# Attention with a mixture of experts on one core: the routed inner layer computed transposed, and the experts' pieces spread one or more to a round

## The chip, the cores and the metric

The kernel runs on one core of a Trainium2 chip. The time is device microseconds of one execution. A core has five instruction streams: PE (TensorE: it multiplies a moving operand by weights that a separate load, PEld, puts into the array), DVE (VectorE), ACT (ScalarE), POOL (GpSimd) and SP (it only issues transfers here). Each runs its own instructions in the order in which the program lists them and waits on the others through semaphores.

## The reference

One layer on 2048 tokens of width 512. `x` is normalised and goes two ways, and both results are added to `x`.

```python
# attention: 16 heads, each with two score maps, causal softmax
attn1, attn2 = softmax(mask(q1 @ k1.T * scale)) @ v, softmax(mask(q2 @ k2.T * scale)) @ v
f = (rfft(attn1, axis=time) - lambda_full * rfft(attn2, axis=time)) * gaussian_filter
attn = rms_norm(irfft(f)) * rms_weight * (1 - LAMBDA_INIT) @ Wout
# feed-forward: 8 experts of inner width 352, each token takes 2, and a shared one of width 704
logits = x @ gate_w.T                       # softmax, top 2, weights renormalised
y_e = (silu(x @ w1[e]) * (x @ w3[e])) @ w2[e]
y = sum over the 2 chosen e of weight * y_e
shared = (silu(x @ sw1) * (x @ sw3)) @ sw2
```

All of it is fp32. One fp32 multiplication shows in the trace as two passes, each a weight load and a matmul; a transpose on PE shows as one.

## The kernel before

The program has three parts: a start (normalisation, gate, queries and keys, and the shared expert of the first four tiles of 128 tokens), `middle` (attention, the rest of the shared expert and the routed experts) and `ending` (the filter in time as products on PE, the projection, the sums). The change touches `middle` almost alone. There PE, DVE, ACT, POOL and SP keep the order in which the Python code emits instructions, so the order is written out by hand.

**Attention as a stream.** Two heads make a group `g` (8 of them), and each has four chunks of 512 queries, `qc` from 3 down to 0. A chunk is a list of units: scores of one head against one block of 128 keys, for both maps, in a PSUM buffer of two banks `ps_s` (there are two such buffers). `Chunk.scores` (L761) lets ACT take the exponential into `pt` (L774), and for blocks on the diagonal POOL clears the upper triangle (L779). `Chunk.values` (L801) multiplies by `v` into `ps_o`; `Chunk.added` (L818) has DVE add up `pt` over the keys. Of a finished chunk, `sums` reduces the added `pt` on PE (`ps_sum`, L827), ACT copies it, and `finish` turns the values and the sums on PE (`ps_ot` L839, `ps_st` L840) and has DVE take the reciprocal (L842) and scale (L847); `put` (POOL, L856) stores the difference of both maps in `vd`. When all four chunks of a group are stored, `folded` does a first butterfly of the filter on POOL in seven steps.

**Rounds.** The stream has 544 units; a round is four, so there are 136, 17 to a group (counted here from round 0). The loop at the end of `middle` does in each round: scores of two units (a first burst), the values of earlier units, `sums` of a chunk that closes, scores of two more units, the other values, `finish`, then pieces of the experts' work, DVE's sums, and steps of `folded`.

**Experts as pieces.** `experts()` is a generator; each `next` emits a piece and yields its estimated PE time, and the round loop takes pieces while `worked / work_all` is behind the round's share. A routed expert works on 128 gathered rows (`xrow`, an indirect transfer that POOL issues two experts ahead), 36 of them in order `j`, with two buffers of up weights (`wu`) and two of down weights (`wd`), which SP refills. It has three pieces: `up_first` (the `w1` half, `xh`, then tanh on ACT L175 and a product on DVE L176), `up_third` (the `w3` half, `xg`, and a product on DVE L182), and a third one that holds the down layer of the expert before (`xy`, L201), this one's inner layer turned back (`ps_u`, L191: three transposes, and two copies by DVE, L193 and L194) and the next one's rows turned (`ps_x`, L159, copied by ACT, L161).

In the up layer (L168) the turned rows `xT` are the weights in the array and 352 columns of `w1` or `w3` move past them, so the result has tokens on the partitions; the down layer needs the inner width there, which is why it is turned back. The shared expert (`hidden`, L231) has the other form already: 128 columns of its weights stay in the array and the tokens move.

`xh`, `xg`, `ps_u`, `ps_x`, `xy`, `ps_sum`, `ps_ot` and `ps_st` share three PSUM buffers (`f_ps`). A new tile takes the buffer that came free first in the program's order, and its first matmul waits until the last reader of that buffer is done.

Of the kernel before, what the change touches and what calls it, by code (L numbers as in the profile page):

```python
# [32 lines left out]
FCH = ((0, 128), (128, 128), (256, 96))  # L33
# [29 lines left out]
def block_kernel(  # L63
# [85 lines left out]
    def expert(mp, fps, yp=None, stores=2, by_scalar=False):  # L149
# [14 lines left out]
        def up_half(w, xT, i, name):  # L164
            dst = bank([P, FI], name)
            for c in range(NE):
                o = (2 * c + i) * FI
                nc.tensor.matmul(dst, xT[:, c, :], w[:, o : o + FI], start=(c == 0), stop=(c == NE - 1))  # L168
            return dst

        def up_first(w, xT):

            h = up_half(w, xT, 0, "xh")
            s = mp.tile([P, FI], F32, tag="s", name="xtanh")
# [13 lines left out]
        def turned_back(u):  # L188
            ps = bank([P, NF, P], "ps_u")
            for ic, (i0, m) in enumerate(FCH):  # L190
                nc.tensor.transpose(ps[:m, ic, :], u[:, i0 : i0 + m], ident)  # L191
            uT = mp.tile([P, NF, P], F32, tag="uT", name="uT")
            nc.vector.tensor_copy(uT[:, :2, :], ps[:, :2, :])  # L193
            nc.vector.tensor_copy(uT[:96, 2, :], ps[:96, 2, :])  # L194
            return uT

        def down_products(pairs):
            y = bank([P, E], "xy")
            for n, (w, uT) in enumerate(pairs):
                for ic, (_, m) in enumerate(FCH):  # L200
                    nc.tensor.matmul(  # L201
                        y, uT[:m, ic, :], w[:m, ic * E : (ic + 1) * E],
                        start=(n == 0 and ic == 0), stop=(n == len(pairs) - 1 and ic == NF - 1),
                    )
            return y
# [9 lines left out]
        def down(pairs, *to):  # L215
            stored(down_products(pairs), *to)

        return up_first, up_third, up, turned_back, (down, down_products, stored), transposed
# [59 lines left out]
    with ExitStack() as pools:  # L278
# [215 lines left out]
        _, _, _, _, (_, _, stored), _ = expert(ep, eps, stores=EARLY)  # L494
# [63 lines left out]
    def middle(general):  # L558


        with ExitStack() as pools:
# [29 lines left out]
            def experts():  # L591
# [5 lines left out]
                _, _, _, _, (_, _, stored), _ = expert(sp, fps, mp, by_scalar=True)  # L597
# [33 lines left out]
                up_first, up_third, _, turned_back, (down, _, _), transposed = expert(rp, fps, mp, by_scalar=True)  # L631
                for i in range(2):
                    fetch_down(es[i], i, nc.sync)
                xT = transposed(xr.pop(0))
                yield 0.5
                for j in range(NR):
                    half = up_first(w_sb[j % 2][0], xT)
                    yield 2.4
# [323 lines left out]
            for i in range(0, len(stream), 4):  # L962
# [7 lines left out]
                while todo:  # L970
                    ended += values()
# [403 lines left out]
```

## Time and profile before

| | us |
|---|---|
| median of 3 runs | 1381.73 (1381.63 to 1382.18) |
| the profiled execution, its own time | 1382.72 |
| its span, first to last instruction | 1380.8 |
| PE busy in it | 1331.9 |
| DVE, ACT, POOL busy | 1005.4, 692.7, 598.3 |
| start / `middle` / `ending`, by the trace | 0 to 253 / 253 to 1263 / 1263 to 1381 |

The routed experts run from about 600 to 1263 us, 18.4 us each. A row of a group gives line, engine, operation, out<-in, shapes and count, then busy time, mean duration of one, and idle time of the engine just before. Matmuls overlap: the mean duration of one is more than what it adds when many follow each other, and the chain (start, length, what) or the starts in the timeline tell what a series takes.

### The profile page before, as it was taken

How to read it: one execution, taken by the hardware profiler on the slowest of the kernel's cores; microseconds unless marked ns; L12 is line 12 of the kernel's file. 1: busy time of each engine (PE TensorE's matmuls, PEld its weight loads, DVE VectorE, ACT ScalarE, POOL GpSimd, SP SyncE). 2: the span in 40 equal slices, each digit the busy share in tenths (PEclk: the TensorE clock that was granted, in tenths of full speed). 3: DMA queues.
4: the chain of work that ended last, by engine and by line, in shares of the span. 5: the costliest groups of instructions: out<-in, count | busy, mean ns of one | idle time of the engine just before them, and what ended most of it. 6: DMA issues, size and time to landing. Idle time of an engine off the chain costs nothing.

```text
span 1380.8 us, 20566 instructions
## 1 busy us (share of the span) xinstructions
PE 1331.9 (96%) x7472; PEld 620.8 (45%) x7472; DVE 1005.4 (73%) x1337; ACT 692.7 (50%) x853; POOL 598.3 (43%) x673
## 2 busy tenths in 40 slices
PE   7999999899999999998899999999999999999998
PEld 3444444333443344444445444544454454445543
DVE  7059881368777776868677888867698779877785
ACT  2311110365656565665566566666667666662321
POOL 0002222012301232136975755757467537632874
PEclk9999999999999999999999999999999999999999
DMA  9406672200210121255455655656656565448996
GB/s 376 167 16 192 189 213 64 87 19 16 78 46 31 47 73 63 81 158 159 149 178 171 200 185 175 179 176 191 200 161 202 190 202 188 170 164 277 179 223 149
DMA packets 74689, 206.58 MB, mean 150 GB/s; under 512 B 12028, under 2 KB 12192, under 8 KB 69200
## 3 DMA queue, kind: packets, MB, share of 16 engines
q1 hardware_dynamic: 61840, 177.62, 39.4%
q0 software_dynamic: 11216, 23.31, 8.1%
q10 hardware_dynamic: 1520, 4.23, 0.9%
q8 instruction: 62, 1.02, 0.3%
q14 instruction: 51, 0.42, 0.1%
HBM read 161.26 MB, written 43.85 MB: 149 GB/s over the span
## 4 chain that ended last, share of the span: by engine, by line
PE 67%; DVE 5%; POOL 3%; DMA 3%; issue 2%; SPq 2%; ACT 2%; ACTq 0%; DVEq 0%; POOLq 0%
PE ps_o L801 17%; PE ps_s L761 12%; PE wh L231 8%; PE xy L201 6%; PE xh L168 6%; PE xg L168 6%; PE wy L269 4%; SPq L669 2%; PE ps_sum L827 2%; DVE sum L818 2%; ACT pt L774 1%; PE po L1196 1%; PE ps_ot L839 1%; PE ps_x L159 1%; DMA kS<-parts_k 1%
## 5 line engine op out<-in xcount | busy, mean ns | idle before, releaser
L818 DVE TENSOR_TENSOR sum<-sum,pt 128x1024 f32<-128x1024 f32 (+2 forms) x576 | 623.4, 1131 | 24.2 <-ACT pt L774 10.7
L774 ACT ACTIVATE pt<-ps_s 128x1024 f32<-128x1024 f32 x544 | 528.1, 1027 | 173.5 <-PE ps_s L761 128.1
L779 POOL TENSOR_SCALAR_AFFINE_SELECT pt<-pt 128x256 f32<-128x256 f32 x256 | 174.9, 708 | 340.5 <-ACT pt L774 277.5
L801 PE MATMUL ps_o<-pt,vd 128*32 128x512 f32 (+3 forms) x2560 | 270.7, 542 | 4.0 <-POOL pt L779 3.9
L761 PE MATMUL ps_s<-qS,kS 64*128 64x512 f32 (+3 forms) x1280 | 209.9, 411 | 14.7 <-ACT pt L774 12.9
L761 PEld LDWEIGHTS ps_s<-qS,kS 64*128 64x128 f32 x1280 | 97.8, 186 | 169.2 <-ACT pt L774 90.2
L231 PE MATMUL wh<-xnT,wu 128*128 128x512 f32 (+1 forms) x352 | 151.4, 578 | 0.0
L801 PEld LDWEIGHTS ps_o<-pt,vd 128*32 128x32 f32 x2560 | 67.2, 110 | 134.5 <-issue 115.5
L473 POOL DMA_INDIRECT who<-pairs,slot x32 | 34.3, 1073 | 202.0 <-DVE pairs L470 100.9
L520 PE MATMUL ps_x<-xnT,wqk_sb 128*128 128x512 f32 x256 | 110.5, 593 | 0.0
L201 PE MATMUL xy<-wd,uT 128*128 128x512 f32 (+1 forms) x216 | 103.5, 616 | 4.0 <-DVE rcp L842 4.0
L231 PEld LDWEIGHTS wh<-xnT,wu 128*128 128x128 f32 x352 | 64.9, 192 | 72.4 <-issue 57.3
L856 POOL TENSOR_TENSOR vd<-o_n 128x128 f32<-128x128 f32 x60 | 37.9, 653 | 137.2 <-DVE o_n L847 129.8
L168 PE MATMUL xh<-wu,xT 128*128 128x352 f32 x288 | 94.5, 471 | 0.7 <-ACT xT L161 0.7
L168 PE MATMUL xg<-wu,xT 128*128 128x352 f32 x288 | 93.2, 466 | 0.0
L520 PEld LDWEIGHTS ps_x<-xnT,wqk_sb 128*128 128x128 f32 x256 | 48.4, 190 | 60.6 <-issue 60.6
L269 PE MATMUL wy<-wd,ws 128*128 128x512 f32 x160 | 73.6, 601 | 0.0
L168 PEld LDWEIGHTS xh<-wu,xT 128*128 128x128 f32 x288 | 52.2, 191 | 33.6 <-issue 7.8
L168 PEld LDWEIGHTS xg<-wu,xT 128*128 128x128 f32 x288 | 52.6, 190 | 32.1 <-issue 4.3
L210 ACT ACTIVATE y_sb<-xy,wcol 128x512 f32<-128x512 f32 x36 | 24.8, 688 | 83.6 <-PE xy L201 83.6
L1052 POOL DMA_INDIRECT res<-ys,slot x32 | 56.6, 1769 | 21.0 <-DMA res<-ysh 10.4
L537 ACT CAST hi<-turned 128x1024 fp32r<-128x1024 f32 x16 | 16.7, 1045 | 93.8 <-DVE turned L535 83.1
(239 smaller groups left out, 1405.3 us busy)
## 6 DMA issues: line engine op xcount, KB each, us to landing
wu<-in_wex_dram SPq DMA_DIRECT2D x40, 1408.0 KB
wd<-in_wex_dram SPq DMA_DIRECT2D x39, 768.0 KB
kS<-parts_k SPq DMA_DIRECT2D x128, 128.0 KB
qS<-parts_q SPq DMA_DIRECT2D x256, 64.0 KB
ys<-y_sb SPq DMA_DIRECT2D x36, 256.0 KB
parts_q<-hi SPq DMA_DIRECT2D x32, 256.0 KB
parts_k<-hi SPq DMA_DIRECT2D x16, 256.0 KB
parts_k<-turned SPq DMA_DIRECT2D x16, 256.0 KB
```

The source lines that it names most:

```text
L168: nc.tensor.matmul(dst, xT[:, c, :], w[:, o : o + FI], start=(c == 0), stop=(c == NE - 1))
L201: nc.tensor.matmul(y, uT[:m, ic, :], w[:m, ic * E : (ic + 1) * E], start=(n == 0 and ic == 0), stop=(n == len(pairs) - 1 and ic == NF - 1),)
L231: nc.tensor.matmul(dst, w_sb[o // WUP][0][:, o % WUP : o % WUP + P], x[:, c, :], start=(c == 0), stop=(c == NE - 1))
L269: nc.tensor.matmul(y, us[i][:, t * P : (t + 1) * P], w_sb[i // NF][1][:, i % NF * E : (i % NF + 1) * E], start=(i == 0), stop=(i == SCH - 1),)
L520: nc.tensor.matmul(ps[:, i, :], wqk_sb[st, qk][:, i, c, :], xnT[:, c, cols], start=(c == 0), stop=(c == NE - 1),)
L761: nc.tensor.matmul(to, k, queries[2 * g + h, qc][r, off : off + w], start=True, stop=not general)
L774: nc.scalar.activation(pt[:, :, used], ps[:, :, used], AF.Exp, scale=SCALE)
L779: nc.gpsimd.affine_select(out=part, in_=part, pattern=[[0, 2], [1, P]], compare_op=ALU.is_ge, fill=0.0, base=0, channel_multiplier=-1,)
L801: nc.tensor.matmul(self.o[r : r + 32, off:], vd[:, kb, v0 : v0 + 32], pt[:, s, :], start=first, stop=self.ended, skip_group_check=True,)
L818: nc.vector.tensor_add(to, to, pt)
L856: eng.tensor_add(vd[:, self.qc * TQ : (self.qc + 1) * TQ, v0 : v0 + 32], self.o_n[:, :, h, 0, :], self.o_n[:, :, h, 1, :],)
L1052: nc.gpsimd.indirect_dma_start(out=came[k], out_offset=None, in_=ys, in_offset=bass.IndirectOffsetOnAxis(ap=slot[:, step - 2, order[k] : o ...
```

## The change

The inner layer of a routed expert is computed transposed. `up_half` keeps 128 columns of `w1` or `w3` in the array and moves the 128 columns of `xT`, for three overlapping column blocks (0, 128 and 224; the down weights of the 32 columns that come twice are zero the second time). Its result has the inner width on the partitions, [128, 3, 128] in place of [128, 352], and goes into the down layer as it is; `turned_back` and its two DVE copies are gone. The third piece turns the next expert's rows first and then does the down layer of the expert before. In the loop, every round takes at least one piece, a round whose first values were those of fewer than two blocks (and in which no chunk closes) takes one between its two bursts of scores, the estimates per piece differ, and a round ahead of one with diagonal blocks does one step of `folded`, not two. The layout of the down weights, prepared on the host, follows the blocks.

```diff
-FCH = ((0, 128), (128, 128), (256, 96))
+FCH = (0, 128, FI - 128)
...
         def up_half(w, xT, i, name):
-            dst = bank([P, FI], name)
-            for c in range(NE):
-                o = (2 * c + i) * FI
-                nc.tensor.matmul(dst, xT[:, c, :], w[:, o : o + FI], start=(c == 0), stop=(c == NE - 1))
+            dst = bank([P, NF, P], name)
+            for ic, i0 in enumerate(FCH):
+                for c in range(NE):
+                    o = (2 * c + i) * FI + i0
+                    nc.tensor.matmul(dst[:, ic, :], w[:, o : o + P], xT[:, c, :], start=(c == 0), stop=(c == NE - 1))
             return dst
...
-        def turned_back(u):
-            ps = bank([P, NF, P], "ps_u")
-            for ic, (i0, m) in enumerate(FCH):
-                nc.tensor.transpose(ps[:m, ic, :], u[:, i0 : i0 + m], ident)
-            uT = mp.tile([P, NF, P], F32, tag="uT", name="uT")
-            nc.vector.tensor_copy(uT[:, :2, :], ps[:, :2, :])
-            nc.vector.tensor_copy(uT[:96, 2, :], ps[:96, 2, :])
-            return uT
...
-        def down_products(pairs):
+        def down_products(w, u):
             y = bank([P, E], "xy")
...
+            for ic in range(NF):
+                nc.tensor.matmul(y, u[:, ic, :], w[:, ic * E : (ic + 1) * E], start=(ic == 0), stop=(ic == NF - 1))
             return y
...
                 for j in range(NR):
                     half = up_first(w_sb[j % 2][0], xT)
-                    yield 2.4
+                    yield 2.8
                     u = up_third(w_sb[j % 2][0], xT, half)
...
-                    yield 2.4
-                    if j > 0:
+                    yield 2.8
+                    if j + 1 < NR:
+                        xT = transposed(xr.pop(0))
+                    if late:
                         down(*late)
                         fetch_down(es[j + 1], (j + 1) % 2, nc.sync)
-                    uT = turned_back(u)
-                    late = [(w_sb[j % 2][1], uT)], ys[j * P : (j + 1) * P, :], wcol[:, j : j + 1]
-                    if j + 1 < NR:
-                        xT = transposed(xr.pop(0))
                     if j == 1:
                         shared.append(True)
-                    yield 3.7
+                    yield 3.2 if late else 0.6
+                    late = w_sb[j % 2][1], u, ys[j * P : (j + 1) * P, :], wcol[:, j : j + 1]
...
-            work_all = (NT - 1 - EARLY) * ((2 * SCH - 1) * 3.45 / TQ + 5.2) + NR * 8.5 - 7.0
+            work_all = (NT - 1 - EARLY) * ((2 * SCH - 1) * 3.45 / TQ + 5.2) + NR * 8.8
...
+            def work():
+                nonlocal worked
+                worked += next(ex, work_all)
...
                 found = burst(units[:2])
-                ended = values()
+                n, ended = values()
                 for c in closing:
                     c.sums()
                     summed += 1
+                if n < 2 and not closing:
+                    work()
                 found += burst(units[2:])
...
-                while worked / work_all < (i + 4) / len(stream):
-                    took = next(ex, None)
-                    if took is None:
-                        break
-                    worked += took
+                while True:
+                    work()
                     added(later[:1])
                     later = later[1:]
+                    if worked / work_all >= (i + 4) / len(stream):
+                        break
...
-                for _ in range(0 if any(map(masked, units)) or not shared else 1 if len(ready) < 2 else 2):
+                if any(map(masked, units)) or not shared:
+                    steps = 0
+                else:
+                    steps = 1 if len(ready) < 2 or any(map(masked, stream[i + 4 : i + 8])) else 2
+                for _ in range(steps):
```

## The prediction

> **What bounds the kernel now.** I read the page first, then stretches of time, then the chain, then the timeline around each PE gap. The page's first two parts say that PE is the bound:
>
> ```profile
> PE 1331.9 (96%) x7472; PEld 620.8 (45%) x7472; DVE 1005.4 (73%) x1337; ACT 692.7 (50%) x853; POOL 598.3 (43%) x673
> ...
> PE   7999999899999999998899999999999999999998
> ```
>
> So the change is worth two things in `middle`: PE work added or removed, and PE gaps filled or opened. The stretches (length, busy time by engine, granted clock, DMA) show how little is idle, and that a gap costs twice: the clock falls after it.
>
> ```profile
> 600.00:800.00 200.00, 187.32 (x1281) 90.99 (x1283) 154.25 (x182) 120.04 (x147) 144.24 (x166) 0.97 0.55 173
> ...
> 770.00:780.00 10.00, 6.93 (x35) 2.34 (x34) 9.86 (x11) 3.53 (x5) 9.29 (x9) 0.83 0.33 87
> 900.00:910.00 10.00, 8.65 (x46) 3.01 (x39) 7.51 (x7) 6.76 (x8) 9.46 (x10) 0.83 0.55 148
> ```
>
> A mean of 0.83 over 10 us is 1.7 us lost, on top of the gap. The chain (start, length, what, count) gives the price of the forms: half an up layer in the old form, the three transposes, and the new form, which the last tile of the shared expert has in `ending` (128 columns of weights in the array, 128 moving):
>
> ```profile
> 844.79 0.33 PE ps_u L191 x3
> ...
> 1233.19 2.37 PE xg L168 x8
> ...
> 1296.19 3.59 PE wh L231 x32
> ```
>
> **The change part by part.**
>
> *Up layer.* A half had 4 products, so 8 passes of 352 columns: 2.37/8 = 0.296 us each. It gets 3x4 products, 24 passes of 128 columns. The 32 passes of the last fence took 0.112 each, with a new weight load for every pass, so a half takes 2.69: +0.32, times 72 halves +23.0. Where scores follow, the old half took 2.56 instead of 2.37 (848.79 on the chain); turned rows followed by scores take 0.53 for four instead of 0.44, so the new form pays such an end too, and I count none.
>
> *Transposes.* 36 x 0.33 = -11.9. The two DVE copies (0.42 and 0.28 by their groups) go; the DVE and ACT operations grow from 352 to 384 columns (by the shared expert's 384 rows 0.557 and 0.492 against 0.52 and 0.465). DVE has 0.63 us less per expert, hidden under PE; if that cover is gone it is a gain.
>
> The Trainium skill, "TensorE: Matmul & The Clock Gate", section "Back-to-back issue gap", speaks against this part: in streams of load and matmul pairs it gives 81 ns per matmul of 128 columns where the isolated gap is 56. If the 25 ns came on top of each of the 1728 new passes, the sum would be some 43 us higher, an estimate from that page; the fence above already is such a stream.
>
> *Rounds without a piece.* I followed the loop by its yields for both kernels. Before, rounds 87, 92, 97 and 102 get none, and then the scores wait for ACT. The timeline of PE at round 87:
>
> ```profile
> 901.20 0.73 PE L761 MATMUL ps_s<-qS,kS 64*128 64x512 f32 x4
> 902.86 0.50 PE L761 MATMUL ps_s<-qS,kS 64*128 64x512 f32 x2 [0.93 <-ACT pt L774]
> 903.78 0.50 PE L761 MATMUL ps_s<-qS,kS 64*128 64x512 f32 x2 [0.41 <-ACT pt L774]
> 904.21 3.25 PE L801 MATMUL ps_o<-pt,vd 128*32 128x512 f32 x16
> ```
>
> Two bursts of 0.67 took from 901.20 to 904.21: 1.67 lost. In the same way 1.71 at 937.41, 1.70 at 975.31 and 1.08 at 1014.29: 6.2. Two were followed by a half-speed window (900 to 910 and 940 to 950, both 0.83): 3.4. After the change every round has a piece: -9.6.
>
> *The piece between bursts.* In round 8 of each group the first values are one block:
>
> ```profile
> 313.24 0.64 PE L801 MATMUL ps_o<-pt,vd 128*32 128x256 f32 x8
> 314.20 0.50 PE L761 MATMUL ps_s<-qS,kS 64*128 64x512 f32 x2 [0.32 <-ACT pt L774]
> 315.11 0.50 PE L761 MATMUL ps_s<-qS,kS 64*128 64x512 f32 x2 [0.42 <-ACT pt L774]
> 315.59 1.06 PE L801 MATMUL ps_o<-pt,vd 128*32 128x512 f32 x8
> ```
>
> Eight such passes take 0.56 (940.45 to 941.01), so 315.59 - 313.80 - 0.67 = 1.1 is lost, seven times, and 0.6 at 941: -8.4. A piece of 2.7 covers it. The same rule acts in round 0, where nothing covers the first exponentials:
>
> ```profile
> 257.87 1.71 PE L761 MATMUL ps_s<-qS,kS 64*128 64x512 f32 x4 [2.23 <-ACT pt L774]
> ```
>
> `wh` moves there: -2.2, and one of two half-speed windows around it (0.81 and 0.85 in 250 to 270), -1.7. Bounds -2 to -5.
>
> *The third piece, turned round.* In a closing round the next free PSUM buffer after `ps_sum`'s is `ps_st`'s, which DVE must have read. Before, in round 69, `xy` came first and covered part of DVE's lag:
>
> ```profile
> 768.02 0.27 PE L840 MATMUL ps_st<-cst,s_sb 128*128 128x128 f32 x1
> 768.13 2.74 PE L201 MATMUL xy<-wd,uT 128*128 128x512 f32 x6
> ...
> 773.13 0.25 DVE L842 RECIPROCAL rcp<-ps_st 128x16 f32<-128x16 f32 x1
> 773.43 0.55 PE L191 MATMUL ps_u<-cst,xtanh 128*128 128x128 f32 x3 [2.56 <-DVE rcp L842]
> ```
>
> Afterwards only the rows (0.44) stand before `xy`, which waits about 4.5 from 768.5; the round takes 7.8 from `ps_st`, not 7.1, and without the transposes should take 6.8: +1.0, and one more half-speed window +1.7. DVE's lighter work does not help, since it idled at 756.49 just before this backlog. Rounds 111 and 119 meet the same order with lags of 1.3 (1111.33 to 1112.63) and 1.6 (1133.63 to 1135.26): +0.75 and +1.1. Together +4.5; bounds 0 (DVE in time) and +17 (rival 3).
>
> *Rounds 51 to 57.* POOL folds without a break from 624 to 682, and PE waits for it:
>
> ```profile
> 682.37 6.68 POOL L779 TENSOR_SCALAR_AFFINE_SELECT pt<-pt 128x256 f32<-128x256 f32 x8
> ...
> 682.83 3.20 PE L801 MATMUL ps_o<-pt,vd 128*32 128x512 f32 x12 [3.01 <-POOL pt L779]
> ```
>
> In the built order POOL has the same operations before these masks in both kernels, so the new limit of one step changes nothing here. The stretch keeps its length, its 4.01 wait at 628 included, and hides what PE gets more in it: 7 x 0.32 - 3 x 0.33 = 1.3. -1.3; bounds 0 and -4 (lighter DVE, quicker POOL).
>
> *The end of `middle`.* Before, one `xg`, two `xy` and the transposes ran after the last scores (1245.36), and the last `put` ended at 1261.58, 16.2 later. Now only the last `xy` is left there. From the same rows (masks until 1248.79, DVE's copies and six sums, `ps_sum` 0.87, reciprocal to `put` 2.2) the `put` comes about 10.9 after the scores: -5.3; the `xg` and `xy` moved ahead cost 2.69 + 2.77: +0.2. The fold after it takes DVE 11 us either way. The last weights of `ending` (chain: 7.11 for `wo_sb` from 1263.33) are issued earlier and stay hidden.
>
> *Queues.* Each piece keeps its transfers: SP's refills follow `xg` and `xy` as before, POOL's gather stays two experts ahead (18 us a round trip, no wait for it before). A piece between bursts puts a refill that waits for PE ahead of later transfers on SP; queries and keys are issued a chunk ahead, so none is late. Nothing is counted.
>
> **Sum.** +23.0 - 11.9 - 9.6 - 8.4 - 3.9 + 4.5 - 1.3 + 0.2 = -7.4. The terms come from an execution of 1382.72 us (span 1380.8), 1.0 above the median and 0.5 above the slowest of the three runs; against the median: 1381.7 - 7.4 = 1374.3.
>
> **Rivals.**
>
> 1. *A larger gain.* DVE, lighter by 23 us, is in time in the closing rounds (-4.5 more), and POOL shares that in rounds 51 to 57 (-4): 1366. For it: POOL waited 2.46 for `o_n` at 633.41. Against: the backlogs start from an idle DVE.
> 2. *The gaps move.* ACT's exponentials must run anyway, and half of the 22 us counted as filled returns elsewhere: +11, 1385. For it: PE is never far ahead of ACT. Against: ACT is busy 66% of 1000 to 1200.
> 3. *Slower by the buffer wait.* If DVE lags by 5 us in every closing round whose piece is rows and `xy` (69, 99, 111, 119), as in 69, the three others add 3.0 to 4 and a window of 1.7 each: about +17, 1391. It decides from 2.5 us more a round. Against: lags there of 0.57 to 1.6.
> 4. *Passes dearer than 0.112.* At 116 ns the change is even, over 118 slower by 0.2%. Nearest rows: 0.110 (transposes, one pass each) and 0.1325 (0.53/4, rows followed by scores), which on all passes would be +35: 1410. Against: 32 passes in a row.
>
> A second rule bears on the windows. The page above, section "What's actually happening", has the clock halve after an idle window of about 3.4 us. The trace disagrees: 1.7 us of waiting was enough around 902. By the page alone those 3.4 us would not be saved, and the sum would be -4.0.
>
> **How the numbers follow.** Forecast 0.50 (own range 1370 to 1379), rival 1 0.13, rival 2 0.17, rival 3 0.12, rival 4 0.08. About 0.2%, 2.8 us, is what a measurement can tell from no change. The forecast and rival 1 are faster (0.63); rival 2 with less than its 11 us is the same (0.12), with all of it slower (0.05); with rivals 3 and 4 slower is 0.25. The range leaves out the far ends of 1, 3 and 4: 1364 to 1388.
>
> **What would show it.** `xh` and `xg` at 2.7 per series of 24 passes, no `ps_u`; no PE wait on ACT `pt` at rounds 8, 25, 42 and so on, nor where the four empty rounds were; a wait of `xy` on DVE `rcp` of over 4 us in round 69; the POOL wait of round 57 still there; `put` some 11 us after the last scores. I am wrong if the series takes 2.8 or more, if waits on `pt` stand elsewhere, or if `xy` waits in every closing round.

## The result and the profile after

The changed kernel takes 1374.7 us (median of 17 runs, 1370.3 to 1380.5) beside 1382.6 for the kernel before (17 runs, 1381.1 to 1387.9): the ratio is 0.9942, 95% interval 0.9928 to 0.9956, or 8 us less. The forecast was 1374.3. The profiled execution of the changed kernel is one of its fastest, 1370.3 with a span of 1368.6, so the two profiles differ by 12.2 in span, 4 more than the medians. That difference is itself something to explain below.

The first part of the page of the changed kernel, busy time by engine, answers to the first lines of the prediction:

```profile
PE 1330.4 (97%) x8516; PEld 695.9 (51%) x8516; DVE 990.0 (72%) x1265; ACT 690.9 (50%) x853; POOL 563.8 (41%) x673
```

PE has 1044 more passes and is busy for the same time (1331.9 before). So something else that counted as busy went away. Here is the up layer, on the chain of the changed kernel (start, length, what, count):

```profile
1227.61 2.68 PE xg L170 x24
```

This is the new half, 24 passes in 2.68, as forecast (2.69). And this is where waits went, from the list of PE's waits between 253 and 1263 (who, waiting for whom: total, times, longest); first before, then after:

```profile
PE ps_s L761 <- ACT pt L774: 12.9, 25, 2.2
PE xy L201 <- DVE rcp L842: 4.0, 1, 4.0
PE ps_o L801 <- POOL pt L779: 3.9, 2, 3.0
PE ps_u L191 <- DVE rcp L842: 2.6, 1, 2.6
```

```profile
PE xy L193 <- DVE rcp L830: 5.8, 4, 3.9
PE ps_r L1067 <- issue: 3.2, 1, 3.2
PE ps_x L159 <- DVE rcp L830: 2.7, 1, 2.7
PE ps_o L789 <- POOL pt L767: 2.7, 3, 1.6
```

The 12.9 us in which scores waited for ACT's exponentials are gone from the list. The waits for DVE's reciprocal changed places (in round 51 `ps_x` waits where `xy` did, in round 69 `xy` where `ps_u` did), and `ending` begins with a wait of 3.2 of its first product (`ps_r`), where before `ps_z` waited 2.3 a little further on. Round 8 of a group (the eighth round below, counted from 0 as in the prediction) now reads like this in PE's timeline (start, length, what), with the piece `wh` between the two bursts of `ps_s`:

```profile
310.25 0.74 PE L749 MATMUL ps_s<-qS,kS 64*128 64x512 f32 x4
310.92 0.64 PE L789 MATMUL ps_o<-pt,vd 128*32 128x256 f32 x8
311.49 3.70 PE L220 MATMUL wh<-xnT,wu 128*128 128x512 f32 x8
315.12 0.74 PE L749 MATMUL ps_s<-qS,kS 64*128 64x512 f32 x4
315.79 1.06 PE L789 MATMUL ps_o<-pt,vd 128*32 128x512 f32 x8
```

The stretches that the prediction showed, in the changed kernel (start:end, length, busy time of PE, PEld, DVE, ACT and POOL with counts, then the granted clock, DMA share, GB/s):

```profile
600.00:800.00 200.00, 190.28 (x1598) 114.63 (x1598) 151.85 (x163) 121.66 (x148) 135.87 (x166) 0.98 0.57 178
770.00:780.00 10.00, 10.00 (x56) 5.01 (x55) 4.09 (x4) 4.89 (x6) 9.48 (x16) 0.81 0.76 218
900.00:910.00 10.00, 10.00 (x84) 6.50 (x87) 7.54 (x6) 6.70 (x9) 9.53 (x9) 1.00 0.75 222
```

The clock is 1.00 where an empty round had made it 0.83 (900 to 910). It is 0.81 behind the wait in round 69.

**The two profiles as a sum.** I took the start-to-start times of all PE instructions in both traces, and set apart what PE was idle and half of the time that it worked at half speed. The 12.2 us are: PE's work +9.5, idle time -10.7, half-speed time -11.0. By the prediction's terms:

| term | predicted | in the two profiles |
|---|---|---|
| up layer, 72 halves | +23.0 | +24.0 |
| transposes | -11.9 | -12.2 |
| scores waiting for exponentials (empty rounds, eighth rounds, round 0), without half-speed time | -16.8 | -16.9 |
| waits in closing rounds | +2.9 | +2.5 |
| POOL's rounds 51 to 57 | -1.3 | -2.2 |
| the end | +0.2 | +2.3 |
| half-speed time | -3.4 | -11.0 |
| all else on PE | 0 | +1.3 |
| sum | -7.4 (rounded) | -12.2 |

Of the 16.9 in the third row, 12.9 are the waits listed above and 3.5 is what the matmuls of scores take less when no wait splits their bursts.

Without half-speed time the forecast was -4.0 and the profiles show -1.2; half-speed time was to give 3.4 and gave 11.0. So the small total came out of a work term that was a little worse and a clock term that was three times as large as foreseen. The experiments are about this split: what the new form costs, what the new loop brings, and why the clock follows.

### The profile page after: what moved, and what is told of

The parts are those of the page before. It is cut to its first block, busy times and chain, and to the rows that moved or that the text cites. A ratio compares the mean times of both kernels' runs of the same rounds, so it can differ in the third digit from the quotient of the medians.

```text
span 1368.6 us, 22652 instructions
## 1 busy us (share of the span) xinstructions
PE 1330.4 (97%) x8516; PEld 695.9 (51%) x8516; DVE 990.0 (72%) x1265; ACT 690.9 (50%) x853; POOL 563.8 (41%) x673
## 4 chain that ended last, share of the span: by engine, by line
PE 70%; DVE 8%; issue 2%; ACT 1%; POOL 1%; DVEq 0%; ACTq 0%
PE ps_o L789 17%; PE ps_s L749 12%; PE wh L220 8%; PE xh L170 7%; PE xy L193 7%; PE xg L170 7%; PE wy L258 4%; DVE sum L806 2%; PE ps_sum L815 2%; PE po L1195 1%; PE ps_x L159 1%; PE ps_ot L827 1%; PE ps_z L1067 1%; DVE sum L803 1%; ACT pt L762 1%
## 5 line engine op out<-in xcount | busy, mean ns | idle before, releaser
L806 DVE TENSOR_TENSOR sum<-sum,pt 128x1024 f32<-128x1024 f32 (+2 forms) x576 | 621.4, 1130 | 32.7 <-ACT pt L762 18.4
L767 POOL TENSOR_SCALAR_AFFINE_SELECT pt<-pt 128x256 f32<-128x256 f32 x256 | 162.6, 659 | 350.0 <-ACT pt L762 284.6
L749 PE MATMUL ps_s<-qS,kS 64*128 64x512 f32 (+3 forms) x1280 | 205.6, 407 | 1.5 <-DVEq L1243 1.2
L844 POOL TENSOR_TENSOR vd<-o_n 128x128 f32<-128x128 f32 x60 | 45.5, 778 | 167.1 <-DVE o_n L835 121.6
L193 PE MATMUL xy<-wd,xtanh 128*128 128x512 f32 x216 | 102.1, 610 | 6.2 <-DVE rcp L830 5.8
L170 PE MATMUL xh<-xT,wu 128*128 128x128 f32 x864 | 104.8, 278 | 0.8 <-ACT xT L161 0.7
L170 PE MATMUL xg<-xT,wu 128*128 128x128 f32 x864 | 105.0, 278 | 0.0
L170 PEld LDWEIGHTS xh<-xT,wu 128*128 128x128 f32 x864 | 99.5, 192 | 10.8 <-issue 4.1
L170 PEld LDWEIGHTS xg<-xT,wu 128*128 128x128 f32 x864 | 99.2, 192 | 9.6 <-issue 9.0
L178 DVE SCALAR_TENSOR_TENSOR xtanh<-xtanh,xh 128x384 f32<-128x384 f32 x36 | 19.9, 554 | 95.8 <-ACT xtanh L177 95.8
L231 DVE SCALAR_TENSOR_TENSOR ws<-ws,wh 128x512 f32<-128x512 f32 (+4 forms) x26 | 16.8, 646 | 63.9 <-ACT ws L230 63.9
## 6 DMA issues: line engine op xcount, KB each, us to landing
ys<-y_sb SPq DMA_DIRECT2D x36, 256.0 KB
parts_q<-hi SPq DMA_DIRECT2D x32, 256.0 KB
parts_k<-hi SPq DMA_DIRECT2D x16, 256.0 KB
parts_k<-turned SPq DMA_DIRECT2D x16, 256.0 KB
```

What stands on the lines that cost most here:

```text
L170: nc.tensor.matmul(dst[:, ic, :], w[:, o : o + P], xT[:, c, :], start=(c == 0), stop=(c == NE - 1))
L193: nc.tensor.matmul(y, u[:, ic, :], w[:, ic * E : (ic + 1) * E], start=(ic == 0), stop=(ic == NF - 1))
L749: nc.tensor.matmul(to, k, queries[2 * g + h, qc][r, off : off + w], start=True, stop=not general)
L767: nc.gpsimd.affine_select(out=part, in_=part, pattern=[[0, 2], [1, P]], compare_op=ALU.is_ge, fill=0.0, base=0, channel_multiplier=-1,)
L806: nc.vector.tensor_add(to, to, pt)
L844: eng.tensor_add(vd[:, self.qc * TQ : (self.qc + 1) * TQ, v0 : v0 + 32], self.o_n[:, :, h, 0, :], self.o_n[:, :, h, 1, :],)
```

## The experiments

Two numbers are read from every run: its time, and the time lost to half speed, which is its span times (1 - mean granted clock). What is left is an estimate of its time at full speed: PE also waits in some of the half-speed time (in the profile of before it works in 15.7 of the 17.9), and the clock is on record in steps of 0.001, which are 1.4 us. Each group ran beside runs of the kernel before on the same chip, and is read against those; the old and the new up layer are called the forms, and "loop" is the new order (a piece in every round, a piece between bursts).

| run | form | loop | median us | before, beside it | ratio (95%) | lost to half speed, median | rest, median |
|---|---|---|---|---|---|---|---|
| before (three groups) | old | old | | 1380.6 / 1384.5 / 1382.0 | 1 | 15.2 / 17.9 / 17.9 | 1363.6 / 1364.9 / 1362.9 |
| changed | new | new | 1374.7 | 1382.6 | 0.9942 (0.9928 to 0.9956) | 9.6 | 1364.5 |
| e1_form_only | new | old | 1381.5 | 1380.6 | 1.0018 (0.9996 to 1.0039) | 7.6 | 1372.3 |
| e2_order_only | old | new | 1360.5 | 1380.6 | 0.9831 (0.9806 to 0.9856) | 8.1 | 1350.5 |
| e3_no_mid | new | no piece between bursts | 1387.1 | 1380.6 | 1.0045 (1.0029 to 1.0061) | 11.1 | 1374.6 |
| e4_down_first | new | new, `xy` before rows | 1371.3 | 1380.6 | 0.9927 (0.9907 to 0.9948) | 4.8 | 1364.8 |
| e5_after_left | new | new, pieces left for the end | 1377.1 | 1384.5 | 0.9942 (0.9921 to 0.9963) | 7.6 | 1366.9 |
| e6_form_dve | new, with copies | old | 1387.9 | 1384.5 | 1.0019 (1.0004 to 1.0033) | 9.7 | 1375.1 |
| e7_old_limit | new | new, old fold limit | 1377.0 | 1384.5 | 0.9948 (0.9926 to 0.9970) | 9.6 | 1366.5 |
| e8_order_one | old | new, one piece in closing rounds | 1361.0 | 1384.5 | 0.9830 (0.9812 to 0.9848) | 9.5 | 1349.6 |
| e9_after_again | new | new | 1374.8 | 1382.0 | 0.9952 (0.9931 to 0.9972) | 7.6 | 1364.9 |
| e10_filler | new | new, four transposes done seven times in round 69 | 1370.8 | 1382.0 | 0.9933 (0.9912 to 0.9954) | 5.5 | 1364.8 |
| e11_always_only | old | no piece between bursts | 1375.4 | 1382.0 | 0.9948 (0.9927 to 0.9968) | 13.7 | 1358.8 |
| e12_order_defer | old | new, loads put off | 1383.5 | 1382.0 | 1.0008 (0.9994 to 1.0023) | 17.9 | 1364.1 |

**The form alone (e1_form_only).** The changed kernel with the loop, the estimates and the order of before:

```diff
-                if n < 2 and not closing:
-                    work()
...
-                while True:
-                    work()
+                while worked / work_all < (i + 4) / len(stream):
+                    took = next(ex, None)
...
-                    if j + 1 < NR:
-                        xT = transposed(xr.pop(0))
-                    if late:
+                    if j > 0:
                         down(*late)
                         fetch_down(es[j + 1], (j + 1) % 2, nc.sync)
+                    if j + 1 < NR:
+                        xT = transposed(xr.pop(0))
```

> The transposed up layer alone, in the schedule of before (its estimates, its loop with rounds that get no piece, the xy ahead of the next rows, the old limit on the folds). My sum: +23.0 for 72 halves in 24 passes and -11.9 for the transposes, -1.3 for what rounds 51 to 57 hide, so +9.8 on before's 1382.6: about 1392 (1389 to 1395). xh and xg take 2.69 per half, the four waits of scores on ACT pt at 901, 937, 975 and 1014 and those of the eighth round of each group stay. Rival A, the form is free or a gain because a lighter DVE returns what PE pays: 1382 or below. Rival B, the passes cost more once scores follow them: 1400 or above.

Measured: +0.9 by the medians, +2.5 by the ratio, where I had +9.8. The theory seemed to have fallen to rival A. But the rest column has +8.7 and the half-speed column -7.6: the form costs PE what its passes say, and the clock gives it back. One place shows it well. Round 87 has the same empty round in both kernels, with the same two waits of scores, 0.93 and 0.41. Its stretch by periods of 3.41 us, first before, then e1_form_only (columns as above):

```profile
901.24:904.66 3.42, 2.07 (x16) 0.78 (x16) 3.38 (x4) 2.87 (x4) 3.18 (x4) 1.00 0.12 39
904.66:908.07 3.41, 3.41 (x20) 0.93 (x12) 3.04 (x3) 0.90 (x1) 3.20 (x3) 0.50 0.80 185
```

```profile
897.71:901.12 3.41, 2.08 (x18) 0.56 (x6) 3.29 (x3) 2.98 (x5) 3.17 (x4) 1.00 0.17 49
901.12:904.53 3.41, 3.40 (x26) 1.35 (x27) 3.41 (x4) 2.37 (x3) 3.18 (x4) 1.00 0.64 143
```

The period with the waits has 2.07 of PE work in one and 2.08 in the other, and only in the first does half speed follow. Elsewhere waits became shorter: where PE waits for POOL (before: 3.01 and 0.91 around 682) more PE work comes ahead and 0.76, 0.29 and 1.58 are left.

**Is it DVE's lighter work? (e6_form_dve)** The two copies per expert put back on the form-only run:

```diff
+                    nc.vector.tensor_copy(u[:, :2, :], u[:, :2, :])
+                    nc.vector.tensor_copy(u[:96, 2, :], u[:96, 2, :])
                     late = w_sb[j % 2][1], u, ys[j * P : (j + 1) * P, :], wcol[:, j : j + 1]
```

> The run with the transposed up layer in the old schedule, and DVE's two copies per expert put back (256 columns on 128 partitions and 128 on 96, of the gated layer onto itself, so that nothing else changes). The form alone cost +0.9 where its passes and transposes give +11. If that was DVE's lighter work, the copies bring 6 us or more back: 1387 to 1392. If it was the clock (PE's added work shortens waits that no longer fill enough of a clock period to halve it), the copies cost nothing: 1380 to 1384, with 5 to 8 us lost to half-speed windows as without them.

The copies last as long as those of before did (groups of DVE by line: count, busy time, mean ns):

```profile
L638 DVE COPY xtanh<-xtanh 128x256 f32<-128x256 f32 x35 | 14.7, 420 | 0.1
...
L639 DVE COPY xtanh<-xtanh 96x128 f32<-96x128 f32 x35 | 9.8, 279 | 0.0
```

The ratio is 1.0019 after 1.0018. The absolute time, 1387.9, lies in the band that I gave for DVE, but the kernel before is also 3.9 slower on this chip than beside e1, so the ratio decides. DVE's relief is not what paid for the form. By the medians, +3.4 after +0.9, and by the intervals of the two ratios, a cost of up to 3.7 cannot be excluded; the 6 or more that the DVE theory asked for can.

**The loop alone (e2_order_only).** The old up layer, with the changed loop and a total equal to the sum of its pieces:

```diff
-            work_all = (NT - 1 - EARLY) * ((2 * SCH - 1) * 3.45 / TQ + 5.2) + NR * 8.5 - 7.0
+            work_all = (NT - 1 - EARLY) * ((2 * SCH - 1) * 3.45 / TQ + 5.2) + NR * 8.5
...
+                if n < 2 and not closing:
+                    work()
                 found += burst(units[2:])
...
-                while worked / work_all < (i + 4) / len(stream):
-                    took = next(ex, None)
+                while True:
+                    work()
...
+                    if worked / work_all >= (i + 4) / len(stream):
+                        break
```

> The new loop alone (a piece in every round, a piece between the bursts where the first values are fewer than two blocks, the planner's total equal to the sum of its pieces, the new limit on the folds), with the up layer, the transposes and the piece sizes of before. The third piece stays xy, transposes back, rows. My sum: -9.6 -8.4 -3.9 +0.2 = -21.7, and round 69 now gets an xh and no xy, so its wait of 3.1 and the window behind it (1.7) go too, unless another closing round takes them up: 1356 to 1362, about 1360. Rival A, the gaps move to other places since ACT's exponentials set the pace: about 1371, with new PE waits on ACT pt or DVE. Rival B, the new form's lighter DVE is what made the closing rounds short: then waits on DVE rcp grow to 10 us or more in the sum and the time is 1368 or above.

1360.5, 20.2 less than before, against about 1360 expected: the terms for the loop hold, and this kernel beats both. (The lower end of the range that I gave, 1356, counted on round 69 as well, 4.8 with its half-speed period. There a wait of 2.3 is left, without half speed behind it, and the new wait below takes back some 4.) The gaps did not move to other scores. A new one of another kind is there, though, in PE's timeline:

```profile
1020.80 0.73 PE L761 MATMUL ps_s<-qS,kS 64*128 64x512 f32 x4
1025.50 5.06 PE L168 MATMUL xh<-wu,xT 128*128 128x352 f32 x8 [3.96 <-DMA wu<-in_wex_dram]
```

`xh` waits 3.96 for its weights, and then runs at half speed (8 passes in 5.06, not 2.37 to 2.56). The prediction had counted nothing for SP's queue.

With e1 this makes a square. The new form costs 0.9 to 2.5 in the old order and, e4 against e2, 13 by the ratios (10.9 by the medians) in the new one; without half-speed time it costs 8.7 and 14.3. So the prediction's +11.1 for the form is about what PE has to do more. It is paid in full where half-speed time is short already (8.1 to 4.8 us), and hardly at all where there is much of it to win back (15.2 to 7.6). These are two points, and not yet a rule.

**The piece between bursts (e3_no_mid).**

```diff
-                if n < 2 and not closing:
-                    work()
                 found += burst(units[2:])
```

> The changed kernel without the piece between the bursts; each round still has a piece. My sum: the waits of the eighth round of each group return (+8.4) and with them the start of round 0 (+2.2, and +1.7 if a half-speed window follows): +10.6 to +12.3, so 1385 to 1387. Rival, the piece only moves a wait to the next burst: +0 to +4, 1375 to 1379.

1387.1: 12.4 more than the changed kernel by the medians, 14 by the ratios (the kernel before was 2 faster beside it), at or a little above the 10.6 to 12.3 that I expected. The waits of the eighth rounds are back in place:

```profile
316.10 0.64 PE L789 MATMUL ps_o<-pt,vd 128*32 128x256 f32 x8
317.11 0.51 PE L749 MATMUL ps_s<-qS,kS 64*128 64x512 f32 x2 [0.37 <-ACT pt L762]
318.03 0.50 PE L749 MATMUL ps_s<-qS,kS 64*128 64x512 f32 x2 [0.41 <-ACT pt L762]
318.50 1.07 PE L789 MATMUL ps_o<-pt,vd 128*32 128x512 f32 x8
```

**Every round a piece, in the old form (e11_always_only).**

```diff
-                if n < 2 and not closing:
-                    work()
```

> The old up layer, with a piece at the end of every round and the total set to the sum of the pieces, without the piece between the bursts. My term for the rounds without a piece is -9.6, and 0 to +2 comes from two pieces moved out of the end: 8 to 10 faster than before, ratio 0.993 to 0.994. The run with both rules was 20.2 faster and the piece between bursts cost 12.4 to take away in the new form, which leaves 7.8. Rival, the waits move to the closing rounds as they did with the new form: 0 to 4 faster, ratio 0.997 or above.

6.6 less by the medians, 7.2 by the ratio: a little under the 8 to 10. Its profile starts with 6.7 of waiting in round 0, and the late weights (2.5) are there too. What is left of e2's gain, 14 to 16, is the piece between bursts in the old form.

**The third piece (e4_down_first).**

```diff
-                    if j + 1 < NR:
-                        xT = transposed(xr.pop(0))
                     if late:
                         down(*late)
                         fetch_down(es[j + 1], (j + 1) % 2, nc.sync)
+                    if j + 1 < NR:
+                        xT = transposed(xr.pop(0))
```

> The changed kernel with the third piece in the old order: xy of the expert before, then the turned rows of the next. In round 69 xy (2.7) then takes the free PSUM buffer and the rows wait some 1.1 for DVE's reciprocal in place of xy's 3.86; in round 119 the wait of 1.5 goes. My terms: -2.7 -1.5, and -1.7 if the half-speed window after round 69 goes too: -4 to -6, about 1369.5. Rival, the wait goes to the next user of the buffer: 0, 1374.7.

1371.3: 3.4 less by the medians, 2 by the ratios, whose intervals overlap, where I had expected 4 to 6. In its profile the wait in round 69 is 1.7 and no half-speed period is left in `middle`, but `xh` now waits for the copy of its rows, which come last:

```profile
PE xh L170 <- ACT xT L161: 3.9, 5, 0.8
...
PE xh L170 <- DMA wu<-in_wex_dram: 2.8, 2, 1.4
...
PE ps_x L159 <- DVE rcp L830: 1.7, 1, 1.7
```

So turning the piece round cost somewhat less than the +4.5 that I counted, because it also saves such waits (3.9 here, 0.7 in the changed kernel). What is won stands in the half-speed column (4.8 after 9.6); the rest is the same (1364.8 after 1364.5).

**The end (e5_after_left).**

```diff
-                    if worked / work_all >= (i + 4) / len(stream):
+                    owed = 8.6 if i >= 480 else 0.0
+                    if worked + owed >= work_all * (i + 4) / len(stream):
                         break
```

> The changed kernel with 8.6 us of pieces (one xh or xg after the other, and one xy) held back over the last 16 rounds, so that they run after the last scores as before. By my sum the end pays what the middle saves: 0, about 1374.7. By the account of the two traces (the change moved 8.5 us of PE work out of the end, but the end became only 4.5 shorter at full clock, because DVE's last sums and the stores behind them are its bound) it is 3 to 4 faster: about 1371. Slower, 1377 or more, if the last pieces put the weights of the ending late as they did before.

1377.1 beside e7_old_limit, which differs from the changed kernel in nothing that matters here, at 1377.0 on the same chip. An `xg` and two `xy` run after the last scores (in the changed kernel one `xy`), the wait of `ps_r` falls from 3.2 to 1.6, and nothing is won or lost that the runs could tell. The 2.3 in the row "the end" of the table stay a reading of two profiles.

**The fold limit (e7_old_limit).**

```diff
-                    steps = 1 if len(ready) < 2 or any(map(masked, stream[i + 4 : i + 8])) else 2
+                    steps = 1 if len(ready) < 2 else 2
```

> The changed kernel with the old limit on the folds: two steps a round as soon as two groups are ready, also ahead of a round with masks. My prediction counted nothing for the limit, since POOL has the same operations before the masks of rounds 57 and 58: 1374.7, and the POOL waits at 677 to 682 stay at 2.7 in all. Rival, the limit is what shortened those waits from 3.9: 1 to 5 slower, with waits of 3 or more there and a half-speed window behind them.

The waits for POOL stay as they were (2.6, longest 1.6) and the ratio is 0.9948 beside 0.9942 and 0.9952: the limit changes nothing here.

```profile
PE ps_s L749 <- ACT pt L762: 4.5, 1, 4.5
...
PE ps_o L789 <- POOL pt L767: 2.6, 3, 1.6
```

The first line is new, one wait of 4.5 for the first exponentials. It is not the edit's: see the last section.

**The same kernel again (e9_after_again).** This run has no edit.

> The changed kernel itself once more, unedited, for a second profile of it beside the next runs. If the scatter of its runs (1370 to 1380) is the clock's, then a wait of the same length costs a half-speed period in one profile and none in the other, by how the wait lies to a grid of 3.41 us periods: the idle part of a period in front of a half-speed one is 1.75 or more, that in front of a full-speed one below 1.9, and the spans of the two profiles differ by about the difference of the time lost to half-speed periods (within 2). If not, the difference sits in longer waits or longer instructions.

Over its 12 runs and the 17 of the first series, a straight line through time against time lost to half speed gives 1.07 us per us lost, with a correlation of 0.69: the clock makes half of the scatter. The two profiles lie 1.6 apart in span, and in half-speed time 2.7, of which 1.0 is behind PE's last work: within the 2 that I allowed. The second one also waits 1.1 for weights, once, where the first does not. In both, full-speed periods with 2.08 or more of idle time had half speed after them, and those with 1.88 or less had not.

**Keeping PE busy in one wait (e10_filler).** The rows of expert 10 are turned seven times over in round 69, in front of the `xy` that waits:

```diff
-        def transposed(x):
+        def transposed(x, times=1):
             ps = bank([P, NE, P], "ps_x")
-            for c in range(NE):
+            for c in list(range(NE)) * times:
...
-                        xT = transposed(xr.pop(0))
+                        xT = transposed(xr.pop(0), 7 if j == 9 else 1)
```

> The changed kernel, with the four transposes of the next rows done seven times in round 69 alone (the same result written again, 24 passes, 2.6 us), so that PE works while xy waits for DVE there. If the clock falls because a period is idle for more than half, xy's wait of 3.86 becomes about 1.2, no half-speed period follows, and round 69 gets 1.7 to 3.4 shorter though PE has more to do: 1.7 to 3.4 less than the changed kernel beside it. If the clock falls for another reason, the half-speed period stays and the time is the same; if the rows' copy, now 2.6 later, holds the next xh, 0 to 2 more.

Here is PE's timeline in round 69, in the changed kernel and in e10_filler:

```profile
763.40 0.60 PE L159 MATMUL ps_x<-cst,xrow 128*128 128x128 f32 x4
767.87 5.49 PE L193 MATMUL xy<-wd,xtanh 128*128 128x512 f32 x6 [3.86 <-DVE rcp L830]
```

```profile
763.89 3.22 PE L159 MATMUL ps_x<-cst,xrow 128*128 128x128 f32 x28
768.38 2.84 PE L193 MATMUL xy<-wd,xtanh 128*128 128x512 f32 x6 [1.26 <-DVE rcp L830]
```

`xy` starts 4.5 after `ps_x` in both, so the 24 repeated passes cost nothing, and then its six passes take 2.84 and not 5.49. The stretch from 760 to 780, for the changed kernel and for e10_filler:

```profile
760.00:780.00 20.00, 16.14 (x119) 8.43 (x107) 13.88 (x16) 8.80 (x12) 17.41 (x22) 0.83 0.48 143
```

```profile
760.00:780.00 20.00, 18.73 (x161) 10.97 (x163) 16.38 (x19) 11.33 (x14) 16.99 (x19) 1.00 0.43 134
```

PE gets through more in the same 20 us: 18.73 busy at a clock of 1.00, not 16.14 at 0.83. The whole run is 4.0 faster than e9 by the medians (2.6 by the ratios, whose intervals overlap); the rest column is the same, and the gain is in the half-speed column. The clock fell because PE was idle, and useless work stopped it. That work was transposes alone: in the period of 3.41 us from 764.13 they are all that PE does, for 2.98, and the clock stays at 1.00.

**Two tries at the late weights.** One piece at most in a closing round (e8_order_one):

```diff
-                    if worked / work_all >= (i + 4) / len(stream):
+                    if closed or worked / work_all >= (i + 4) / len(stream):
```

> The run with the new loop and the old up layer (1360.5), with at most one piece at the end of a round after a chunk's sums. There xh waited 3.96 at 1021 for its weights, which come late behind the next group's keys and queries, because two pieces stood in round 102; now it comes a piece later. My expectation: -4.0 for the wait and -1.7 to -3.4 for the clock behind it, 1353 to 1356. Rival, another piece meets the late weights: 1358 to 1361.

1361.0, ratio 0.9830 after 0.9831: my expectation was wrong and its rival right. `xh` moves by a piece and still waits 3.06 for `wu`. What stands ahead of that refill can be seen in e2's SP timeline (start, length, what, count):

```profile
991.54 12.24 SPq L681 DMA_DIRECT2D qS<-parts_q  x8
1003.83 2.40 SPq L669 DMA_DIRECT2D kS<-parts_k  x4
1007.58 2.47 SPq L141 DMA_DIRECT2D wu<-in_wex_dram  x1
```

The row of eight loads of queries lasts 12.2, and the refill of `wu` is behind it. The next expectation calls all of it issuing, but SP's list of waits says otherwise (who, waiting for whom: total, times, longest):

```profile
SPq L681 <- DMA kS<-parts_k: 6.0, 2, 3.7
...
SPq L681 <- DMA wd<-in_wex_dram: 1.8, 1, 1.8
...
SPq L681 <- DMA ys<-y_sb: 0.3, 1, 0.3
```

In 8.1 of the 12.2 SP waits until transfers that it issued earlier have landed; the eight loads themselves last 3.9 in all.

So the loads of queries and keys were put behind the pieces of the round (e12_order_defer):

```diff
-                            load_queries(*turns[n + 1])
+                            loads.append((load_queries, turns[n + 1]))
...
+                while loads:
+                    f, a = loads.pop(0)
+                    f(*a)
```

> The run with the new loop and the old up layer, with the loads of the next chunk's queries and keys put behind the round's pieces on SP instead of at the chunk's first burst. There SP spent 12.2 on issuing queries from 991.5, and the weights for xh came 3.96 late at 1021. If that queue is the cause, the wait and the half-speed period behind it go: 4 to 7 less, ratio 0.978 to 0.980. Rival, keys or queries come late in the short chunks, or the weights are late anyway: ratio 0.983 or above, with PE waits on kS or qS.

The rival holds, and more than I had feared: no wait for weights is left, and the scores wait for queries instead, 18.4 us in seven waits. (The row below has one more, 1.6 at 255; e2 has that one too, under another name.) Held up by the queries, PE also comes later to the weights, so this run does not show that SP's queue alone had made them late. The whole gain of the loop is gone.

```profile
PE ps_s L761 <- DMA qS<-parts_q: 20.0, 8, 6.4
```

## Why the prediction was right, and where its terms were not

**Up layer, +23.0: right.** 0.112 per pass held: +24.0 in the profiles, and the same +0.31 per half whatever stands behind it (2.37 to 2.68 before rows or `xg`, 2.46 to 2.77 and 2.56 to 2.88 before scores). The Trainium skill's figure for load and matmul pairs ("TensorE: Matmul & The Clock Gate", "Back-to-back issue gap"), which by the prediction's estimate would have added some 43, did not apply on top: the trace's own series of 32 was the better price. Rival 4 is out.

**Transposes, -11.9: right** (-12.2). That DVE's share of them is hidden was only argued; in the old order e6 finds 3.7 at most, of the copies' 24.5, that is not hidden.

**Rounds without a piece, the piece between bursts, round 0: right.** 16.8 of waiting was to go and 16.9 went; e2 (20.2 for the loop, expected 21.7), e3 (12.4 to 14, expected 10.6 to 12.3) and e11 (6.6 to 7.2, expected 8 to 10) price them one by one. Rival 2, that half of it returns elsewhere, is out: no wait of scores on exponentials of 0.1 us or more is left in the profile after.

**Third piece turned round, +4.5: right in place, a little too large.** `xy` waits 3.86 in round 69 (I said about 4.5), 1.48 in 119 (1.1), 0.18 in 111 (0.75); undoing it gives 2 to 3.4 back. Rival 3 needed that lag in all four rounds, and rounds 99 and 111 have 0.33 and 0.18. Rival 1 needed DVE to be in time in them, which in 69 it is not.

**Rounds 51 to 57, -1.3: right in kind.** The waits there did not keep their length: the two around 628 and 682 fell from 7.9 to 5.7 in all. That is 2.2, between my bounds of 0 and -4.

**The end, +0.2: too good by 2.1 in the profiles.** I had taken an `xg` and an `xy` as moved ahead; an `xh` went too, since in the kernel before one starts as the last scores end (1245.29). The last `put` ends 12.1 after the last scores (1239.43 to 1251.49), not 10.9. `ending` begins with a wait of 3.2 (`ps_r`) in place of one of 2.3 (`ps_z`), with less of PE's work left to cover it; that is 0.9 of the 2.3, and the others are small waits further on. e5 could not measure this term.

**Half-speed time, -3.4: the step that failed.** I counted the half-speed periods next to the waits that I took away, and one more behind round 69. What came back is larger: the runs of before lose 15 to 18 and those of the changed kernel 7.6 to 9.6; side by side on one chip it is 8.3 (e7) and 10.3 (e9). In periods, the profile of before has ten, and that of after three, without the last one at the program's end. I had counted on two fewer. The other five that went are the second one of round 0, two around 631, one at 683 and one of the two in `ending`. I kept the other waits at their length and their half-speed periods with them; in fact a wait that gets shorter by 1 can lose its whole period: 4.01 became 2.71 at 628, where the clock was 0.5 for two periods before and stays at 1.00 in the profile after, and 3.01 and 0.91 became 0.79, 0.29 and 1.58 around 680, again with one half-speed period before and none after. Here is the stretch around 631 before, by periods (the last section has the one after):

```profile
628.18:631.59 3.41, 0.13 (x1) 0.00 (x0) 3.41 (x5) 0.00 (x0) 2.69 (x4) 1.00 0.18 61
631.59:635.00 3.41, 2.67 (x3) 1.18 (x4) 3.28 (x6) 0.00 (x0) 1.59 (x2) 0.50 0.16 55
```

So it was luck that the total came within 0.4 us of the median: two misses met. Work and waits gave -1.2 in the profiles where I had -4.0, and +1.6 to +2.0 in the rest column of runs on one chip (e7, e9), that is nothing or a little loss, while the clock gave all of the 7 or 8 us that were measured. Why the empty rounds of the new form were seldom followed by half speed, with the same waits, stays open.

## What to carry to other kernels

Price a change of form in the schedule in which it will live. In this kernel the same 11 us of PE work cost 1 to 2.5 in an order with many waits and 15 us of half-speed time to win back, and 11 to 13 in one with few, so a form and an order that are changed together should each be tried alone. Here the order alone, with the old form, is the best version (1360.5; ratio 0.9831; e8 is equal to it), 14 to 15 below the change as it was made. Count each wait of PE with what the clock takes after it, and if a long one cannot be covered by useful work, cover it with work already done.

## What the runs showed of the hardware

**The clock is decided by periods.** In all profiles half speed starts at steps of 3.41 us, whatever the kernel does, and lasts one period or a few. I summed PE's idle time in each such period that ran at full speed from 20 us on, over 14 profiles, without the last period of each program. Idle for 1.97 or more: half speed followed 35 times in 35. Idle for 1.75 to 1.96: 12 in 20. Idle for 0.85 to 1.74: 4 in 80, three of them in or beside empty rounds, with 1.6 to 1.8 of scores in the period. The Trainium skill ("TensorE: Matmul & The Clock Gate", "What's actually happening") says that the window is 3413 ns and free-running, and the steps agree; it has the clock fall after an idle window, and these rows say that a little over half of one is enough. What counts beside idle time in the periods of scores, no run here tells.

So the same wait costs 1.7 us or nothing, by how it lies to the grid. The wait of 2.7 and 0.3 in round 51, in the changed kernel and in e7_old_limit (columns as before):

```profile
627.03:630.44 3.41, 1.53 (x14) 1.34 (x12) 3.31 (x6) 0.00 (x0) 1.32 (x2) 1.00 0.30 76
630.44:633.86 3.42, 2.26 (x8) 1.29 (x9) 3.35 (x7) 0.58 (x1) 1.51 (x2) 1.00 0.26 93
633.86:637.27 3.41, 3.41 (x23) 1.04 (x25) 1.92 (x3) 2.13 (x3) 3.23 (x7) 1.00 0.16 51
```

```profile
634.21:637.62 3.41, 2.24 (x21) 2.05 (x19) 3.31 (x5) 0.67 (x1) 1.96 (x3) 1.00 0.68 149
637.62:641.04 3.42, 1.54 (x6) 0.91 (x7) 3.35 (x8) 0.58 (x1) 0.80 (x2) 1.00 0.19 68
641.04:644.45 3.41, 3.41 (x5) 1.01 (x3) 2.13 (x2) 0.00 (x0) 3.31 (x6) 0.50 0.24 84
```

PE works 1.53 and 2.26 in the two periods of the first and stays at 1.00; it works 2.24 and 1.54 in those of the second and falls to 0.50. This is near the edge, where either happens.

**The first exponentials of `middle` come early or late.** ACT's timeline in the changed kernel and in e7_old_limit:

```profile
256.16 1.94 ACT L762 ACTIVATE pt<-ps_s 128x1024 f32<-128x1024 f32 x2 [23.65 <-DMA qS<-parts_q]
```

```profile
261.93 1.94 ACT L762 ACTIVATE pt<-ps_s 128x1024 f32<-128x1024 f32 x2 [29.10 <-DMA who<-pairs,slot]
```

5.8 us apart, with the same program up to there. In the profiles of before, of the changed kernel and of e1 to e4, e9 and e10 ACT starts between 256.0 and 257.1, in those of e5 to e8, e11 and e12 between 260.9 and 261.9, each time with a transfer named as what released it. When it is late PE waits 2.9 to 8.0 and a half-speed period comes with it, in whichever kernel it happens. It may be the other part of the scatter of the runs, which only the profiled executions could show; what holds the transfers up was not tried.

**A queue waits for what it issued before.** In e2 eight small loads take 12.2 us on SP's row, of which 8.1 are waits until earlier transfers have landed, each time the one issued eight before it, whose semaphore the load also uses. A refill of weights was issued behind them, and PE waited 3.96 for it. With the loads moved behind that refill (e12) no wait for weights is left, and the loads are late by 18.4 in all. Whether another assignment of semaphores would free the queue was not tried.
